# Network vectors on the common load queue, and a first result laid out by channel, sample and position

## The chip, the cores and the metric

The kernel runs on one core of one Trainium2 chip. The metric is the device time of one execution in microseconds (us), as a median of runs. The core has the engines PE (matrix products; PEld is its weight load), DVE, ACT and POOL (elementwise work), and SP, which here only issues transfers. ACT can issue transfers too. All transfers run on the same 16 DMA engines, and their queues are told apart in the profile as q1 (issued by SP), q10 (issued by ACT) and q8 (instructions).

## The reference

Two layers follow each other. Each normalizes its input over groups, makes a set of convolution weights of its own for every sample b and position l by a small network from z, applies them along l with three taps, and adds the input.

```python
S2, B, CI, CO, L, K, A, H = (32, 32, 64, 64, 256, 3, 16, 128)
h = jax.nn.relu(_ln(z @ W1 + b1, g1, be1))
w = (h @ W2 + b2).reshape(B, L, CI, CO, K)
hb = jax.nn.relu(_ln(z @ Wb1 + bb1, gb1, beb1))
bias = (hb @ Wb2 + bb2).transpose(0, 2, 1)
...
out = jnp.einsum('sbilk,bliok->sbol', x_uf, w)
out = out + bias[None]
...
x = x + _L0_conv_ref(_gn(x), ...)
x = x + _L1_conv_ref(_gn(x), ...)
```

`_gn` takes mean and variance over 32 groups of positions, across b and all channels. So layer 1 cannot normalize anything before all of layer 0's result is there. Everything is float32.

## The kernel before

**Tiling.** A unit u is one b of one layer: u = 0 to 31 is layer 0, u = 32 to 63 layer 1. A chunk v = 2u + h is half of a unit's output channels, so a layer has 64 chunks. In each chunk PE first makes the convolution weights (`make`, L390 and L391: the network's vectors `hT` of the unit against the table `w2`), DVE and ACT move them with their bias to `wall` (`take`, L401 and L416), and later PE multiplies them with the normalized input `xn` (`products`, L433). The products of a chunk stand on PE behind the first `make` of the following chunk. DVE adds the products to the residual (L442), in layer 0 it also takes statistics of the sum (L445), and the result is stored.

**What is loaded for each chunk, and in what order.** `after(v)` stands behind the products of chunk v. It issues on SP: the store of the chunk (layer 0: four transfers to `x1`, L367, in runs of 64 numbers, 256 B; layer 1: one to `out`, L372); the residual of chunk v + 2 (`load_residual`; layer 0: one transfer, L140; layer 1: four from `x1`, L143, in runs of 256 B); the next half of a unit's input, two channels by position parity in layer 0 (`load_pairs`, L128, runs of 8 KB) and twice 64 channels in layer 1 (L131, and L132 shifted by one position; runs of 1024 and 1020 B); and the bias of chunk v + 2 spread over samples (`load_bias`, L354, four transfers, runs of 8 KB). In between, POOL normalizes the half that was loaded before (L380, two instructions) and adds the bias to the residual of chunk v + 1 (L361). `load_pairs` waits for the first of these in layer 1, and `load_bias` for the last, since there is one buffer of each.

**`hT`.** The vectors of unit u + 1 are loaded by ACT (L116) at the head of chunk 2u, two buffers in turn. ACT executes in order, so the transfer is issued when ACT has done all `take` work of chunk 2u - 1.

**Completion counters.** Each transfer of SP and ACT signals one of eight semaphores, DMAHW0 to DMAHW7, which the scheduler deals out in turn over both queues. Before a transfer is issued, its engine waits until the transfer that had the same semaphore before (eight earlier in the scheduler's order) is complete.

## Time and profile before

| | us |
|---|---|
| median of 3 runs | 4618.15 (4603.26 to 4620.66) |
| profiled execution | 4594.6 |
| its span on the core | 4592.5 |
| first statistics and networks | to about 295 |
| first store of layer 0 (L367) | 328.20 |
| first store of layer 1 (L372) | 2400.46 |
| last two stores of layer 1, first of them | 4558.35 |

The span starts with the first instruction. A place in time is given in us from there. "Issue" as the cause of a wait means that the engine waited for nothing that the profile shows. PEclk is the share of the full clock that PE was granted. A chunk is told by the time from one chunk's first store to the next one's, since SP issues one group of stores a chunk.

### The profile page before, as it was taken

Reading aid. Unit: us, or ns where it says so; the run is one execution under the profiler, and the core shown is the slowest. Engines: PE = TensorE matmul, PEld = TensorE weight load, DVE = VectorE, ACT = ScalarE, POOL = GpSimd, SP = SyncE. Lnnn points to the kernel's source line nnn. Section 1 sums busy time; section 2 is a strip of 40 time slices with the busy share of each in tenths; the row PEclk is TensorE's granted clock in tenths of the full one; section 3 lists DMA queues with packets and bytes.
Section 4 is the critical chain, followed back from the end, with each engine's and each line's share of the span. In section 5 each row is a group of like instructions: output and inputs, shape, how many; then the busy total and the mean of one; then the engine's idle time right before and its main releaser. Section 6 shows DMA issues by size and latency. Waiting matters only on the chain.

```text
span 4592.5 us, 193878 instructions
## 1 busy us (share of the span) xinstructions
PE 4069.4 (89%) x90704; PEld 3883.6 (85%) x90704; DVE 2642.2 (58%) x3168; ACT 1291.2 (28%) x4264; POOL 2074.9 (45%) x618
## 2 busy tenths in 40 slices
PE   6889999999999999999969888888888888888888
PEld 3569999999999988899868888888888888888888
DVE  6876666666666666666645454545444554454455
ACT  3432232332322322223222222222222222222222
POOL 3465544455444554445344353353443533534532
PEclk9689999999999999999989999999999999999999
DMA  8874444445444454444567667576576675765764
GB/s 307 330 239 133 142 142 133 133 133 148 146 142 124 124 150 142 130 126 133 160 162 165 143 151 170 134 166 152 134 173 141 153 169 134 168 157 137 174 148 107
DMA packets 760621, 718.23 MB, mean 156 GB/s; under 512 B 567492, under 2 KB 715016, under 8 KB 716296
## 3 DMA queue, kind: packets, MB, share of 16 engines
q1 hardware_dynamic: 724488, 683.80, 56.5%
q10 hardware_dynamic: 35328, 22.03, 1.7%
q8 instruction: 709, 11.62, 1.1%
q14 instruction: 96, 0.79, 0.1%
HBM read 558.93 MB, written 146.80 MB: 154 GB/s over the span
## 4 chain that ended last, share of the span: by engine, by line
PE 82%; issue 9%; DVE 3%; DMA 3%; POOL 2%; ACT 1%; ACTq 0%; SPq 0%; POOLq 0%; DVEq 0%
PE pg L390 48%; PE pc L433 23%; PE pg L391 10%; DVE wall L401 2%; POOL sq L198 1%; DMA bd<-bs 1%; PE p L186 1%; DMA zt<-in_L_conv_z_dram 1%; DVE parts L445 1%; DVE room L442 1%; DMA room<-x 1%; PE p L226 0%; ACT ht L216 0%; ACT sq L190 0%; PE p L213 0%
## 5 line engine op out<-in xcount | busy, mean ns | idle before, releaser
L391 PE MATMUL pg<-hT,w2t 128*64 128x128 f32 x24576 | 2808.4, 278 | 60.7 <-issue 60.6
L390 PE MATMUL pg<-hT,w2t 128*64 128x128 f32 x24576 | 2808.6, 278 | 56.5 <-issue 48.2
L390 PEld LDWEIGHTS pg<-hT,w2t 128*64 128x64 f32 x24576 | 2758.8, 140 | 82.3 <-issue 61.9
L391 PEld LDWEIGHTS pg<-hT,w2t 128*64 128x64 f32 x24576 | 2759.2, 140 | 60.7 <-issue 60.7
L401 DVE TENSOR_TENSOR wall<-pg,b 128x1024 f32<-128x1024 f32 (+1 forms) x1536 | 1869.0, 1220 | 870.7 <-PE pg L391 866.8
L416 ACT ACTIVATE wall<-pg,b 64x128 f32<-64x128 f32 x4096 | 1176.7, 481 | 3090.3 <-DVE wall L401 2224.6
L380 POOL TENSOR_TENSOR xn<-room,gmean 128x2048 f32<-128x2048 f32 x128 | 606.6, 4739 | 2205.5 <-DMA room<-x 1104.4
L433 PE MATMUL pc<-wall,xn 128*32 128x128 f32 (+2 forms) x40960 | 1047.4, 261 | 313.3 <-issue 288.9
L433 PEld LDWEIGHTS pc<-wall,xn 128*32 128x32 f32 x40960 | 988.9, 114 | 379.1 <-issue 351.9
L442 DVE TENSOR_TENSOR room<-pc,room 128x512 f32<-128x512 f32 x512 | 354.1, 692 | 1002.4 <-PE pc L433 883.7
L380 POOL TENSOR_TENSOR xn<-xn,rstd 128x2048 f32<-128x2048 f32 x128 | 782.5, 6113 | 10.0
L361 POOL TENSOR_TENSOR room<-room,bt 128x2048 f32<-128x2048 f32 x128 | 593.4, 4636 | 82.3 <-DMA bt<-bd 72.3
L445 DVE BATCH_NORM_STATS2 parts<-room 128x6 f32<-128x256 f32 x512 | 192.9, 418 | 8.7
L198 POOL TENSOR_TENSOR sq<-sq 128x512 f32<-128x512 f32 (+2 forms) x192 | 103.6, 540 | 156.1 <-ACT sq L190 143.6
L186 PE MATMUL p<-wc,zt 17*128 17x256 f32 x256 | 99.8, 553 | 39.3 <-DMA zt<-in_L_conv_z_dram 39.3
L186 PEld LDWEIGHTS p<-wc,zt 17*128 17x128 f32 x256 | 67.5, 277 | 63.1 <-issue 39.7
L213 PEld LDWEIGHTS p<-ident,hs 128*128 128x128 f32 x256 | 50.2, 223 | 49.9 <-issue 49.9
L226 PE MATMUL p<-ht,Wb 128*64 128x512 f32 x64 | 56.7, 985 | 20.5 <-ACT ht L216 20.2
L213 PE MATMUL p<-ident,hs 128*128 128x128 f32 x256 | 62.7, 426 | 3.7 <-DVE hs L204 3.7
L287 DVE BATCH_NORM_STATS2 parts<-xn 128x6 f32<-128x256 f32 x192 | 64.0, 409 | 0.0
L287 DVE BATCH_NORM_STATS2 parts<-spare 128x6 f32<-128x256 f32 x160 | 53.5, 412 | 0.0
L287 DVE BATCH_NORM_STATS2 parts<-room 128x6 f32<-128x256 f32 x160 | 53.5, 412 | 0.0
(44 smaller groups left out, 231.4 us busy)
## 6 DMA issues: line engine op xcount, KB each, us to landing
bt<-bd SPq DMA_DIRECT2D x512, 256.0 KB, 8.9
room<-in_xp_dram SPq DMA_DIRECT2D x64, 1024.0 KB, 8.2
room<-in_xs_dram SPq DMA_DIRECT2D x64, 1024.0 KB, 6.4
x<-room SPq DMA_DIRECT2D x256, 256.0 KB, 4.2
room<-x SPq DMA_DIRECT2D x64, 1024.0 KB, 9.2
room<-x SPq DMA_DIRECT2D x256, 256.0 KB, 5.4
out_dram<-room SPq DMA_DIRECT2D x64, 1024.0 KB, 5.9
room<-x SPq DMA_DIRECT2D x64, 1020.0 KB, 12.9
```

The source lines that it names most:

```text
L186: nc.tensor.matmul(self.p1[:, k], self.zt[:, k * P : (k + 1) * P], self.t["wc"], start=True, stop=True)
L198: nc.gpsimd.tensor_tensor(to, self.sq[:, :, 0:w], self.sq[:, :, w : 2 * w], ALU.add)
L287: nc.vector.bn_stats(parts[:, g, u, h, :], xv[q % NX][:, j, :, g * E : (g + 1) * E])
L361: nc.gpsimd.tensor_tensor(y, y, bts.pop(v), ALU.add)
L380: nc.gpsimd.tensor_tensor(o, i, b, op)
L390: nc.tensor.matmul(pg[0:C, k, :], w[:, k0 * C : (k0 + 1) * C], h0, start=True, stop=True)
L391: nc.tensor.matmul(pg[C:P, k, :], w[:, k1 * C : (k1 + 1) * C], h1, start=True, stop=True)
L401: nc.vector.tensor_tensor(place(rows, a), pg[rows].rearrange("p o (t m) -> p t m o", t=NT), b2[n][rows, kind, None, None, o0 : o0 + OG].to ...
L416: nc.scalar.activation(place(rows, 0)[:, :, :, k], pg[rows, k].rearrange("p (t m) -> p t m", t=NT), AF.Identity, bias=b2[n][rows, kind, o0 ...
L433: nc.tensor.matmul(pc[t * S : (t + 1) * S, n0 - q * EB : n1 - q * EB, :], xn[:, u % 2, t * MT + p + 1, :], wall[:, t, a : a + (n1 - n0) * CH],
L442: nc.vector.tensor_tensor(part, pc.rearrange("p n o -> p o n"), part, ALU.add)
L445: nc.vector.bn_stats(parts[:, 2 * q + g, u, h, :], part[:, :, g * E : (g + 1) * E])
```

## The change

The `hT` transfer moves from ACT's queue to SP's, and from the head of chunk 2u (for unit u + 1) to `after(2u + 1)` (for unit u + 2), behind the residual loads and ahead of `load_pairs`. The first two units are loaded ahead of the loop. `x1` is laid out as channel, sample, position instead of sample, channel, position. Layer 1's `load_pairs` then reads 64 runs of 16 KB (the second transfer 4 B less, shifted by one number) instead of 1024 runs of about 1 KB. The last number of each sample's shifted row is then the next sample's first; it stands at an odd position, and `normalize` in layer 1 reads even ones only. The stores to `x1` and the residual loads keep their runs of 256 B, with 32 KB between consecutive channels and 1 KB between samples, where it was 1 KB and 64 KB.

```diff
-    x1 = [dram.tile([S, C, L], FP, name=f"x1_{b}") for b in range(B)]
+    x1 = [dram.tile([C, S, L], FP, name=f"x1_{b}") for b in range(B)]
...
     def load_hidden(u):
         h = hp.tile([P, 2, M], FP, tag="hT", name="hT")
-        nc.scalar.dma_start(out=h, in_=hd[u // 2][u % 2].rearrange("p (a m) -> p a m", a=2))
+        nc.sync.dma_start(out=h, in_=hd[u // 2][u % 2].rearrange("p (a m) -> p a m", a=2))
...
-            src = x1[u - B][k * SH : (k + 1) * SH].rearrange("s c l -> c s l")
+            src = x1[u - B][:, k * SH : (k + 1) * SH, :].rearrange("c s l -> c (s l)")
+            t = t.rearrange("p s l -> p (s l)")
             nc.sync.dma_start(out=t[0:C], in_=src)
-            nc.sync.dma_start(out=t[C:P, :, 0 : L - 1], in_=src[:, :, 1:L])
+            nc.sync.dma_start(out=t[C:P, 0 : SH * L - 1], in_=src[:, 1 : SH * L])
...
-                    in_=x1[u - B][:, h * CH : (h + 1) * CH, t * LT : (t + 1) * LT],
+                    in_=x1[u - B][h * CH : (h + 1) * CH, :, t * LT : (t + 1) * LT].rearrange("o s l -> s o l"),
...
-                        out=x1[u][:, h * CH : (h + 1) * CH, t * LT : (t + 1) * LT],
+                        out=x1[u][h * CH : (h + 1) * CH, :, t * LT : (t + 1) * LT].rearrange("o s l -> s o l"),
...
+            if h == 1 and u + 2 < U:
+                hs[u + 2] = load_hidden(u + 2)
             if v + 1 == NH * B:
...
-        hs[0] = load_hidden(0)
+        for u in range(2):
+            hs[u] = load_hidden(u)
...
-            if h == 0 and u + 1 < U:
-                hs[u + 1] = load_hidden(u + 1)
```

How this moves instructions. First SP in layer 0, before, from the input load of one chunk to the residual load of the next; behind each transfer stand the semaphores that it waits for.

```order
L128 DMA room<-in_xp_dram 128x2048 [waits DMAHW0_49,Pool_49]
L354 DMA bt<-bd_146 32x2048 [waits DMAHW2_49,DMAHW1_49,Pool_49]
L354 DMA bt<-bd_146 32x2048 [waits DMAHW3_49]
L354 DMA bt<-bd_146 32x2048 [waits DMAHW4_49]
L354 DMA bt<-bd_146 32x2048 [waits DMAHW5_49]
L367 DMA x_20_92<-room 32x32x64 [waits DMAHW6_49,DVE_49]
L367 DMA x_20_92<-room 32x32x64 [waits DMAHW7_49]
L367 DMA x_20_92<-room 32x32x64 [waits DMAHW0_49]
L367 DMA x_20_92<-room 32x32x64 [waits DMAHW1_49]
L140 DMA room<-in_xs_dram 128x2048 [waits DMAHW2_49]
```

The turn goes 0, 1, (2), 3, 4, 5, 6, 7, 0, 1, 2: the four bias loads have 1, 3, 4 and 5, and the 2 between them went to ACT's `hT`. So the residual load at the end, whose turn is 2 again, waits until that `hT` transfer is complete. On ACT, before, there are 64 pieces of `take` work (two chunks) between one `hT` and the next:

```order
L116 DMA hT<-hd_109 128x256
L416 ACTIVATE wall<-pg,b_0_184 64x4x32 x64
L116 DMA hT<-hd_109 128x256
L416 ACTIVATE wall<-pg,b_0_184 64x4x32 x64
L116 DMA hT<-hd_110 128x256
```

After the change ACT has none of these transfers in the loop, and on SP, in the same stretch of layer 0, from the residual load of one chunk to that of the next, it reads:

```order
L141 DMA room<-in_xs_dram 128x2048 [waits DMAHW6_49]
L116 DMA hT<-hd_114 128x256 [waits DMAHW7_49,PE_49]
L128 DMA room<-in_xp_dram 128x2048 [waits DMAHW0_49,Pool_49]
L355 DMA bt<-bd_146 32x2048 [waits DMAHW1_49,Pool_49]
L355 DMA bt<-bd_146 32x2048 [waits DMAHW2_49]
L355 DMA bt<-bd_146 32x2048 [waits DMAHW3_49]
L355 DMA bt<-bd_146 32x2048 [waits DMAHW4_49]
L368 DMA x_20_92<-room 32x32x64 [waits DMAHW5_49,DVE_49]
L368 DMA x_20_92<-room 32x32x64 [waits DMAHW6_49]
L368 DMA x_20_92<-room 32x32x64 [waits DMAHW7_49]
L368 DMA x_20_92<-room 32x32x64 [waits DMAHW0_49]
L141 DMA room<-in_xs_dram 128x2048 [waits DMAHW1_49]
```

The turn is whole on SP, and the residual load waits for the first bias load, eight transfers earlier on its own queue. `hT` itself waits for PE: its buffer was last read by the `make` of chunk 2u + 1. In layer 1, SP before, from one chunk's store to its input loads:

```order
L372 DMA out_dram<-room 128x2048 [waits DMAHW6_49,DVE_49]
L143 DMA room<-x_14_86 32x32x64 [waits DMAHW7_49]
L143 DMA room<-x_14_86 32x32x64 [waits DMAHW0_49]
L143 DMA room<-x_14_86 32x32x64 [waits DMAHW1_49]
L143 DMA room<-x_14_86 32x32x64 [waits DMAHW2_49]
L131 DMA room<-x_15_87 64x16x256 [waits DMAHW3_49,Pool_49]
L132 DMA room<-x_15_87 64x16x255 [waits DMAHW4_49]
```

And after the change, in a chunk that also loads `hT`:

```order
L373 DMA out_dram<-room 128x2048 [waits DMAHW2_49,DVE_49]
L144 DMA room<-x_12_84 32x32x64 [waits DMAHW3_49]
L144 DMA room<-x_12_84 32x32x64 [waits DMAHW4_49]
L144 DMA room<-x_12_84 32x32x64 [waits DMAHW5_49]
L144 DMA room<-x_12_84 32x32x64 [waits DMAHW6_49]
L116 DMA hT<-hd_126 128x256 [waits DMAHW7_49,PE_49]
L132 DMA room<-x_13_85 64x4096 [waits DMAHW0_49,Pool_49]
L133 DMA room<-x_13_85 64x4095 [waits DMAHW1_49]
```

`hT` stands ahead of the two input loads, and these have lost a dimension: 64 rows of 4096 and 4095 numbers.

## The prediction

> **What bounds the kernel now.** I read the page's busy time and chain first, then what PE waits for, stage by stage.

> ```profile
> PE 4069.4 (89%) x90704; PEld 3883.6 (85%) x90704; DVE 2642.2 (58%) x3168; ACT 1291.2 (28%) x4264; POOL 2074.9 (45%) x618
> PE 82%; issue 9%; DVE 3%; DMA 3%; POOL 2%; ACT 1%; ACTq 0%; SPq 0%; POOLq 0%; DVEq 0%
> PE   6889999999999999999969888888888888888888
> ...
> q8 instruction: 709, 11.62, 1.1%
> ```

> PE is the bound. Beside its own work the chain holds 9% "issue", in which PE waits for nothing that the profile shows. PE is less busy (8 instead of 9 tenths) in the second half, layer 1. The waits of PE, in two windows of 59 chunks of layer 0 and 58 of layer 1, first the windows' sums:

> ```profile
> 451.74:2330.92 1879.18, 1749.08 (x41526) 1711.33 (x41522) 1197.99 (x1422) 549.33 (x1894) 868.50 (x171) 0.97 0.47 137
> 2462.01:4500.89 2038.88, 1770.52 (x40842) 1725.65 (x40840) 1005.62 (x929) 526.98 (x1856) 884.62 (x175) 0.95 0.67 154
> ```
> ```profile
> PE pc L433 <- issue: 119.4, 50, 6.3
> ...
> PE pc L433 <- issue: 159.9, 96, 6.1
> PE pg L391 <- issue: 60.6, 24, 4.5
> PE pg L390 <- issue: 47.6, 17, 4.6
> ```

> Columns of the windows: length, busy time (and count) of PE, PEld, DVE, ACT, POOL, then the granted clock, the DMA share and GB/s. A chunk has 704 matmuls, so 41526 and 40842 are 59 and 58 chunks: **31.85 us a chunk in layer 0, 35.15 in layer 1**. The first wait row is layer 0's, the other three are layer 1's: 119 and 268 us. The DMA engines are busy 0.47 of the time in layer 0 and 0.67 in layer 1.

> What is "issue"? In layer 1's products:

> ```profile
> 3147.03 1.74 PE L433 MATMUL pc<-wall,xn 128*32 128x32 f32 x63
> 3150.14 2.86 PE L433 MATMUL pc<-wall,xn 128*32 128x128 f32 x128 [1.38 <-issue]
> 3159.10 5.06 PE L433 MATMUL pc<-wall,xn 128*32 128x128 f32 x129 [6.09 <-issue]
> ```

> PE stops every 128 matmuls. PE has 2 x 90704 records and q8 moved 11.62 MB, so about 64 B an instruction; 128 matmuls with their 128 weight loads are 16.4 KB, which is also q8's mean packet (11.62 MB / 709). So I read these stops as PE waiting for its next packet of instructions, late because the 16 DMA engines are full of the kernel's own transfers. Products use up a packet in 2.9 us, `make` in about 6 (60 matmuls in 3 us, in the last row of the rates below), so a burst of transfers hurts most when it meets products.

> When do the bursts come? SP's waits (first row layer 0's window, second layer 1's), then SP's queue over two chunks of layer 1, and ACT's `hT`:

> ```profile
> SPq L140 <- DMA hT<-hd: 481.7, 28, 18.0
> ...
> SPq L143 <- DMA hT<-hd: 595.0, 29, 22.4
> ```
> ```profile
> 3093.29 0.36 SPq L372 DMA_DIRECT2D out_dram<-room  x1
> 3093.70 23.09 SPq L143 DMA_DIRECT2D room<-x  x4
> 3116.89 2.17 SPq L131 DMA_DIRECT2D room<-x  x1
> ...
> 3120.31 2.90 SPq L354 DMA_DIRECT2D bt<-bd  x4
> 3123.31 0.37 SPq L372 DMA_DIRECT2D out_dram<-room  x1
> 3123.72 15.95 SPq L143 DMA_DIRECT2D room<-x  x4
> ```
> ```profile
> 3111.91 0.33 ACTq L116 DMA_DIRECT2D hT<-hd  x1
> ```

> Once a unit, the residual loads wait 17 to 21 us on average for an `hT` that ACT issues only behind two chunks of its own work (3111.91). The semaphores dealt out in turn over both queues make this wait, no data does. In these 20 us the DMA engines lie idle beside `make`; then everything is issued at once (3116.9 to 3123.7) into the products and on top of the next chunk's load. What that costs is seen by single chunks:

> ```profile
> 362.28:392.22 29.94, 28.92 (x708) 27.99 (x706) 20.16 (x24) 9.59 (x32) 29.78 (x6) 1.00 0.49 143
> ...
> 422.04:451.74 29.70, 28.98 (x710) 28.08 (x706) 20.16 (x24) 9.61 (x32) 29.54 (x6) 1.00 0.49 144
> 1206.64:1238.56 31.92, 28.85 (x706) 28.13 (x702) 20.15 (x24) 9.04 (x32) 1.10 (x2) 0.99 0.47 136
> 1238.56:1268.52 29.96, 29.96 (x712) 29.75 (x712) 20.34 (x24) 9.41 (x32) 29.80 (x6) 0.95 0.50 146
> 2432.20:2462.01 29.81, 28.91 (x705) 28.06 (x701) 17.34 (x17) 9.09 (x32) 23.03 (x5) 1.00 0.80 179
> 3093.29:3123.31 30.02, 29.48 (x726) 29.06 (x722) 18.28 (x17) 9.06 (x32) 5.21 (x2) 1.00 0.41 104
> 3123.31:3164.92 41.61, 30.22 (x692) 29.11 (x690) 16.40 (x17) 9.05 (x32) 26.01 (x6) 0.92 0.84 185
> 4500.89:4529.36 28.47, 28.47 (x710) 28.22 (x708) 17.33 (x17) 9.06 (x32) 11.20 (x3) 1.00 0.48 113
> ```

> The first two rows are the first and last of three chunks of layer 0 before a residual load first waits for an `hT`: 29.82 us on average. From then on they alternate, in the middle of the layer 31.92 and 29.96. Chunk 2432.20 is the key: layer 1, **all 5 MB of its transfers, none held back, 29.81 us**. With the same transfers piled up, the pair at 3093.29 takes 30.02 + 41.61. The last row, with no input load (POOL and DMA nearly idle later on), is layer 1's floor: 28.47.

> SP's queue in the key chunk:

> ```profile
> 2432.20 0.36 SPq L372 DMA_DIRECT2D out_dram<-room  x1
> 2432.60 6.84 SPq L143 DMA_DIRECT2D room<-x  x4
> 2439.55 1.03 SPq L131 DMA_DIRECT2D room<-x  x1
> ...
> 2446.95 1.92 SPq L354 DMA_DIRECT2D bt<-bd  x4
> ```

> **The change part by part.**

> *`hT` on SP.* The wait of the residual loads goes, in all chunks after the first few. I take the observed chunks for what is left: layer 0 59 x (31.85 - 29.82) = **120 us**, layer 1 58 x (35.15 - 29.81) = **310 us**. A check from the other side: at the three early chunks' PE busy time of 28.9 the layer-0 window would have 59 x 28.9 = 1705 instead of 1749 (44 less, the time at a reduced clock), and 79 or so of 119 us of issue go (at 0.7 a chunk left): 123. What is late next: in layer 0 DVE (20.16 busy of 29.8), since 29.82 holds it already; in layer 1 products meet the tail of the bias load, which 29.81 holds too. What it adds: 64 issues on SP of 0.33 us behind the residual loads, covered as long as SP has gaps (5 us ahead of the bias loads in the key chunk). `hT` now waits for PE at chunk 2u + 1's `make`; that stands ahead of the products whose result the store ahead of it on SP already waited for, so it adds nothing for the input and bias loads behind it. It is there over a unit ahead of its use. If that cover were gone, PE would stop for a landing of about 2 us.

> *16 KB runs.* Rates, by windows with one kind of transfer each: 8 KB runs into 128 partitions, 8 KB runs into 32 (the bias), 256 B stores, and the 1 KB loads into 64 partitions:

> ```profile
> 1230.00:1234.00 4.00, 3.80 (x169) 3.53 (x160) 3.38 (x9) 0.00 (x0) 0.00 (x0) 1.00 1.01 424
> 1255.00:1258.00 3.00, 3.00 (x60) 3.00 (x58) 2.13 (x2) 1.35 (x6) 2.92 (x2) 1.00 1.07 232
> 1209.00:1212.00 3.00, 2.80 (x52) 2.56 (x50) 2.06 (x3) 1.89 (x8) 0.00 (x0) 1.00 0.89 219
> 2443.00:2446.00 3.00, 3.00 (x60) 3.00 (x56) 1.95 (x3) 2.27 (x8) 3.00 (x1) 1.00 1.07 206
> ```

> The 2.1 MB of a chunk's input take 10.2 us at 206 GB/s. The new shape is in no row. It is between 232 (long runs, few partitions: 9.0 us) and 424 (long runs, all partitions: 4.9 us). I take the nearer, 232, since 256 B, 1 KB and 8 KB runs all give 206 to 232 where a transfer covers a part of the partitions: 1.2 us fewer of DMA in a chunk, of which I count **0**, because they fall beside `make`. At 424 the transfers would end ahead of the products, and a chunk would come near the floor.

> [...]

> *The pitch of the 256 B runs.* Same bytes and runs at other addresses; the trace has no such row. The nearest slow one also writes 256 B runs, in the first stage (the second row; the first is the store to `x1`; size and median us to landing):

> ```profile
> x<-room SPq DMA_DIRECT2D x256, 256.0 KB, 4.2
> ...
> bd<-bs ACTq DMA_DIRECT2D x32, 128.0 KB, 9.2
> ```

> It lands 5 us later, at half the size; at that price layer 1's bias, behind these loads, would end 5 us later and reach into the products, which is rival 2's time. The other end is 424 GB/s, rival 1's. I take 219 and 0 us, since three very different patterns share 206 to 232 and the slow row is from another stage. SP's issue of the input loads has 64 rows instead of 1024 (1.03 us before, 0.36 for a store of 128 rows): about 1 us of SP, hidden.

> **Sum.** 120 + 310 + 2 (the first chunk of layer 1) = 432 us. The profiled execution took 4594.6 (span 4592.5), so 4162.6. It is 0.5% below the median of the runs, 4618.15; scaled by that ratio: **4184 us**.

> **Rivals.**
> 1. *The input arrives at the full rate* (424 GB/s). For: run length grows 16-fold. Against: 8 KB runs at 232. Layer 1 at its floor, 28.47: 58 x 6.68 = 387, with 122 from the rest 509; 4594.6 - 509 = 4086, scaled 4107.
> 2. *Only half of layer 1's piling goes*, because input and bias are still issued together and reach into the products (5 MB need 23 of 30 us). For: DMA share 0.80 in the key chunk. Against: that chunk itself. At 32 us a chunk: 183 + 122; 4290, scaled 4312.
> 3. *Long runs hold instruction packets up.* If a DMA engine finishes a long run before it turns to q8, PE stops in `make` too. The input lasts 9 us, 1.5 packets of `make`, so two stops a chunk; layer 1's longest stop in `make` is 4.6. At that price 29.8 + 9.2 = 39.0: layer 1 loses 223, layer 0 gains 120, 4698, scaled **4722, slower**. It decides from 35.15 + 120/58 = 37.2 us a chunk, 3.7 us a stop. For: nothing here ran 16 KB runs beside `make`. Against: 8 KB runs beside it cost nothing (chunk 422.04, 1.00 clock). At half the price: 34.4, about 4450.
> 4. *It isn't when, it is how much*: PE's stops depend on the bytes, which don't change, and the time stays at 4618. For: layer 1 has more bytes and more stops. Against: key chunk. [...]

> **How the numbers follow.** Chances: forecast 0.52, rival 1 0.20, rival 2 0.12, rival 3 0.05 at full and 0.04 at half price, rival 4 0.07. The forecast's own spread is 4154 to 4230 (29.3 to 30.6 us a chunk in layer 1). The range reaches from below rival 1 to rival 2, **4095 to 4315**, and leaves out 16% and tails. Faster by over 0.5% (23 us, about what a measurement here can tell): 0.52 + 0.20 + 0.12 + 0.04 = 0.88; slower 0.05; the same 0.07.

> **What would show it.** Right: no wait of residual loads for `hT` in SP's waits; chunks evenly 29.5 to 30 us in both layers; issue waits of PE under 50 us in each window; clock 0.99 or more. 16 KB step: the windows with input loads alone say 232 or 424. Rival 3 would show as issue waits at L390 and L391 while the input is loaded; rival 2 as waits at L433 beside a late bias load. I am wrong if even chunks still have stops.

## The result, and the profile after

| | before | after |
|---|---|---|
| median, us | 4617.26 (4603.26 to 4620.66, 4 runs) | 4304.34 (4300.02 to 4309.94, 4 runs) |
| ratio, 95% interval | | 0.9328 [0.9306, 0.9351] |
| span of the profiled execution, us | 4592.5 | 4303.7 |

The kernel is 6.7% faster. The spans differ by 288.8 us. By the first stores of chunks, as before, they come from these stretches:

| stretch | before, us | after, us | difference |
|---|---|---|---|
| to the first store of layer 0 | 328.20 | 325.39 | -2.8 |
| next four chunks | 123.54 | 120.87 | -2.7 |
| 59 chunks of layer 0 | 1879.18 | 1765.19 | -114.0 |
| to the third store of layer 1 | 131.09 | 139.59 | +8.5 |
| 58 chunks of layer 1 | 2038.88 | 1861.82 | -177.1 |
| rest | 91.6 | 90.8 | -0.8 |

A chunk of layer 0 now takes 1765.19 / 59 = **29.92 us**, a chunk of layer 1 1861.82 / 58 = **32.10 us**. First the page of the changed kernel, busy time and chain:

```profile
PE 3955.2 (92%) x90704; PEld 3758.3 (87%) x90704; DVE 2637.9 (61%) x3168; ACT 1294.4 (30%) x4264; POOL 2083.3 (48%) x618
PE 82%; issue 6%; DVE 6%; DMA 2%; POOL 2%; ACT 1%; SPq 0%; ACTq 0%; POOLq 0%; DVEq 0%
```

"Issue" fell from 9% to 6% of the chain, and PE is 114 us less busy at the same number of matmuls, while the granted clock in the two windows rose from 0.97 and 0.95 to 1.00. The two windows of the changed kernel (length, busy time and count of PE, PEld, DVE, ACT, POOL, granted clock, DMA share, GB/s):

```profile
446.26:2211.45 1765.19, 1713.94 (x41526) 1666.57 (x41522) 1190.31 (x1416) 550.62 (x1888) 871.50 (x171) 1.00 0.52 148
2351.04:4212.86 1861.82, 1696.69 (x40838) 1648.63 (x40835) 1005.65 (x929) 527.51 (x1856) 889.10 (x175) 1.00 0.73 168
```

PE's waits in them (total us, times, longest), the first row layer 0's, the others layer 1's:

```profile
PE pc L434 <- issue: 37.9, 74, 2.6
...
PE pc L434 <- issue: 143.8, 138, 2.5
PE pg L392 <- issue: 11.3, 14, 1.3
PE pg L391 <- issue: 9.9, 12, 1.8
```

Layer 0's issue went from 119 to 38 us. Layer 1's went from 268 to 165; the waits in `make` fell to a fifth (108 to 21), those in the products are more in number and shorter (96 of 1.7 us on average before, 138 of 1.0 us now). SP's waits in layer 1:

```profile
SPq L373 <- DVE room L443: 1081.6, 59, 22.0
SPq L355 <- POOL room L362: 148.2, 29, 5.4
SPq L116 <- PE pg L392: 23.6, 28, 1.1
```

No residual load waits for `hT` any more. SP waits where it has nothing to do yet (the store, for its data), and `hT` waits for PE 0.8 us a time. So the wait that the change was to remove is gone in every unit, and yet layer 1 keeps over half of its issue. One chunk shows how, first SP's queue, then every microsecond from the end of `make`:

```profile
3089.85 0.36 SPq L373 DMA_DIRECT2D out_dram<-room  x1
3090.25 6.78 SPq L144 DMA_DIRECT2D room<-x  x4
3097.13 0.99 SPq L116 DMA_DIRECT2D hT<-hd  x1
3098.22 0.45 SPq L132 DMA_DIRECT2D room<-x  x1
3098.72 0.59 SPq L133 DMA_DIRECT2D room<-x  x1
3104.57 1.71 SPq L355 DMA_DIRECT2D bt<-bd  x4
```
```profile
3102.00:3103.00 1.00, 1.00 (x22) 1.00 (x20) 0.72 (x1) 1.00 (x6) 1.00 (x1) 1.00 1.05 213
3103.00:3104.00 1.00, 1.00 (x22) 1.00 (x20) 0.76 (x1) 0.33 (x2) 1.00 (x1) 1.00 1.03 213
...
3111.00:3112.00 1.00, 0.85 (x30) 0.58 (x22) 0.00 (x0) 0.00 (x0) 0.03 (x1) 1.00 0.99 213
3112.00:3113.00 1.00, 0.00 (x0) 0.00 (x0) 0.00 (x0) 0.00 (x0) 1.00 (x1) 1.00 1.02 229
3113.00:3114.00 1.00, 0.19 (x8) 0.19 (x12) 0.00 (x0) 0.00 (x0) 1.00 (x1) 1.00 0.76 156
3114.00:3115.00 1.00, 1.00 (x41) 1.00 (x37) 0.32 (x1) 0.00 (x0) 1.00 (x1) 0.57 0.22 57
3115.00:3116.00 1.00, 1.00 (x28) 0.92 (x20) 0.37 (x1) 0.00 (x0) 1.00 (x1) 0.50 0.02 8
```

The transfers begin at once and in good order, and the 16 DMA engines are full for 23 us, to 3114 (a share of 0.90 to 1.11 in the windows from 3090 to 3113). `make` ends near 3110. The products run into the tail of the bias load, PE stops for 2 us (3111.9 to 3113.8), and then works some 3 us at a clock of 0.57 to 0.50. The first two rows, between the landing of the residual and the issue of the bias, show the input load in its 16 KB runs: 213 GB/s.

### The profile page after: what moved, and what is told of

The parts are those of the page before. It is cut to its first block, busy times and chain, and to the rows that moved or that the text cites. A ratio compares the mean times of both kernels' runs of the same rounds, so it can differ in the third digit from the quotient of the medians.

```text
span 4303.7 us, 193876 instructions
## 1 busy us (share of the span) xinstructions
PE 3955.2 (92%) x90704; PEld 3758.3 (87%) x90704; DVE 2637.9 (61%) x3168; ACT 1294.4 (30%) x4264; POOL 2083.3 (48%) x618
## 3 DMA queue, kind: packets, MB, share of 16 engines
q8 instruction: 709, 11.62, 1.2%
## 4 chain that ended last, share of the span: by engine, by line
PE 82%; issue 6%; DVE 6%; DMA 2%; POOL 2%; ACT 1%; SPq 0%; ACTq 0%; POOLq 0%; DVEq 0%
PE pg L391 52%; PE pc L434 23%; PE pg L392 6%; DVE wall L402 3%; POOL sq L199 1%; DMA zt<-in_L_conv_z_dram 1%; DVE parts L446 1%; DVE room L443 1%; PE p L187 1%; POOL xn L381 1%; DMA room<-x 1%; ACT ht L217 0%; ACT sq L191 0%; DMA hd<-ht 0%; DMA xn<-in_xs_dram 0%
## 5 line engine op out<-in xcount | busy, mean ns | idle before, releaser
L391 PE MATMUL pg<-hT,w2t 128*64 128x128 f32 x24576 | 2729.0, 273 | 22.1 <-issue 11.1
L392 PE MATMUL pg<-hT,w2t 128*64 128x128 f32 x24576 | 2729.3, 273 | 11.9 <-issue 11.7
L391 PEld LDWEIGHTS pg<-hT,w2t 128*64 128x64 f32 x24576 | 2677.4, 137 | 45.4 <-DVE wall L402 24.8
L392 PEld LDWEIGHTS pg<-hT,w2t 128*64 128x64 f32 x24576 | 2677.4, 137 | 16.8 <-issue 16.7
L434 PE MATMUL pc<-wall,xn 128*32 128x128 f32 (+2 forms) x40960 | 1017.5, 255 | 218.0 <-issue 191.0
L434 PEld LDWEIGHTS pc<-wall,xn 128*32 128x32 f32 x40960 | 949.0, 111 | 294.3 <-issue 266.3
## 6 DMA issues: line engine op xcount, KB each, us to landing
bt<-bd SPq DMA_DIRECT2D x512, 256.0 KB, 10.2
x<-room SPq DMA_DIRECT2D x256, 256.0 KB, 4.3
room<-x SPq DMA_DIRECT2D x256, 256.0 KB, 6.1
```

The source lines that it names most:

```text
L391: nc.tensor.matmul(pg[0:C, k, :], w[:, k0 * C : (k0 + 1) * C], h0, start=True, stop=True)
L392: nc.tensor.matmul(pg[C:P, k, :], w[:, k1 * C : (k1 + 1) * C], h1, start=True, stop=True)
L434: nc.tensor.matmul(pc[t * S : (t + 1) * S, n0 - q * EB : n1 - q * EB, :], xn[:, u % 2, t * MT + p + 1, :], wall[:, t, a : a + (n1 - n0) * CH],
```

## The experiments

Layer 0 and layer 1 below are the mean times of a chunk in the profiled execution, by first stores, where 31.85 and 35.15 stand for before and 29.92 and 32.10 for the change. All ratios are to the kernel before, run on the same chip.

| | median, us | ratio, 95% interval | layer 0, us | layer 1, us |
|---|---|---|---|---|
| e1 `hT` alone | 4301.69 | 0.9317 [0.9299, 0.9335] | 29.96 | 31.90 |
| e2 layout alone | 4622.23 | 1.002 [1.0001, 1.0039] | 31.87 | 35.35 |
| e3 two ahead, ACT's queue | 4463.77 | 0.9667 [0.9648, 0.9685] | 30.21 | 34.55 |
| e4 1020 B runs | 4318.69 | 0.935 [0.9332, 0.9369] | 30.02 | 32.18 |
| e5 no bias loads in layer 1 | 4225.01 | 0.9166 [0.9134, 0.9199] | 29.90 | 30.72 |
| e6 1 MB more a chunk | 4354.90 | 0.9454 [0.9427, 0.9481] | 30.77 | 32.0 |
| e7 2 MB more a chunk | 4536.45 | 0.9849 [0.9814, 0.9884] | 33.59 | 31.94 |
| e8 second copy, shifted | 4598.80 | 0.9984 [0.9966, 1.0003] | 37.33 | 29.03 |
| e9 two equal copies | 4248.79 | 0.92 [0.9176, 0.9223] | 30.43 | 30.51 |
| e10 the change again | 4312.06 | 0.9329 [0.9305, 0.9354] | 30.04 | 32.12 |
| e11 e9, bias first | 4177.14 | 0.9053 [0.9034, 0.9071] | 30.37 | 29.29 |
| e12 the change, bias first | 4339.85 | 0.9398 [0.938, 0.9416] | 29.97 | 32.63 |

### Which part of the change does it: e1, e2, e3, e4

e1 is the kernel before with `hT` as in the change:

```diff
-        nc.scalar.dma_start(out=h, in_=hd[u // 2][u % 2].rearrange("p (a m) -> p a m", a=2))
+        nc.sync.dma_start(out=h, in_=hd[u // 2][u % 2].rearrange("p (a m) -> p a m", a=2))
...
+            if h == 1 and u + 2 < U:
+                hs[u + 2] = load_hidden(u + 2)
...
-        hs[0] = load_hidden(0)
+        for u in range(2):
+            hs[u] = load_hidden(u)
...
-            if h == 0 and u + 1 < U:
-                hs[u + 1] = load_hidden(u + 1)
```

> The kernel before with hT alone moved to SP, two units ahead; x1 keeps its layout and the input loads their 1 KB runs. Theory A (the run length is worth nothing, since 64-partition loads stay at 206 to 232 GB/s, and layer 1's 32.1 us a chunk come from the bias load's tail meeting the products): within 0.5% of the full change, 4290 to 4325 us, layer 1 at 32 us a chunk. Theory B (the 16 KB runs hold PE's instruction packets up and give part of the gain back): 29.8 us a chunk in layer 1 as in the one unhindered chunk of before, so some 130 us less than the full change, 4150 to 4200 us. Theory C (the long runs do help): slower than the full change, above 4330 us.

e2 is the change with those same lines put back to what they were, so that only the layout and the runs differ.

> The full change with hT left where it was (ACT, one unit ahead). Theory A: the residual loads keep their wait of about 20 us for hT and the piled transfers their stops: within 0.5% of before, 4595 to 4640 us. Theory B: slower than before by up to 2.3 us a chunk of layer 1, 4640 to 4750 us. Theory C: faster than before, under 4590 us.

Measured: e1 0.9317, the change 0.9328, and their intervals overlap; e2 1.002. **All of the gain is `hT`'s, none of it the layout's.** e2 alternates in layer 1 between 29.80 and 40.9 us, and SP waits there as before, now at L144:

```profile
SPq L144 <- DMA hT<-hd: 582.9, 29, 22.0
```

e3 keeps `hT` two chunks ahead, but issues it on ACT's queue:

```diff
-        nc.sync.dma_start(out=h, in_=hd[u // 2][u % 2].rearrange("p (a m) -> p a m", a=2))
+        nc.scalar.dma_start(out=h, in_=hd[u // 2][u % 2].rearrange("p (a m) -> p a m", a=2))
```

> The full change, but hT stays on ACT's queue, issued at the new place (two units ahead, behind the first piece of take work). Tells the place from the queue. If the late issue behind two chunks of ACT's work was what held SP, the early place alone mends it: 4290 to 4325 us, no SP wait for hT above 2 us. If semaphores shared by two queues hold SP whatever the place, a wait for hT stays in SP's list and the time lies between the two kernels, 4400 to 4600 us.

Measured: 4463.77, half of the gain. SP's waits in layer 0 and in layer 1 (one window each), and one chunk's bias loads on SP's queue:

```profile
SPq L368 <- DMA hT<-hd: 742.6, 28, 27.2
...
SPq L355 <- DMA hT<-hd: 666.5, 26, 27.1
```
```profile
3201.42 27.41 SPq L355 DMA_DIRECT2D bt<-bd  x4
```

Nobody needs this `hT` soon, and SP still waits 27 us for it, because a transfer of SP's has its semaphore next in turn. With the transfer's new place in the program the turn falls on the store (layer 0) and the bias load (layer 1) instead of the residual load. In layer 0, where it is the store that waits, this costs little (30.21 us a chunk); the loss is layer 1's (34.55). So the harm lies in one turn over two queues of which one lags, not in how early the data are wanted.

e4 is the change with layer 1's input read in 1020 B runs from the new layout:

```diff
-            src = x1[u - B][:, k * SH : (k + 1) * SH, :].rearrange("c s l -> c (s l)")
-            t = t.rearrange("p s l -> p (s l)")
-            nc.sync.dma_start(out=t[0:C], in_=src)
-            nc.sync.dma_start(out=t[C:P, 0 : SH * L - 1], in_=src[:, 1 : SH * L])
+            src = x1[u - B][:, k * SH : (k + 1) * SH, :]
+            nc.sync.dma_start(out=t[0:C, :, 0 : L - 1], in_=src[:, :, 0 : L - 1])
+            nc.sync.dma_start(out=t[C:P, :, 0 : L - 1], in_=src[:, :, 1:L])
```

> The full change with layer 1's input loaded from the new layout in runs of 1020 B again (16 a row; the first transfer leaves out each sample's last, unread number too). Theory A: as the full change, 4290 to 4325 us. Theory B: 4150 to 4200 us. With e1 it also tells the layout's pitch: if e1 and this one differ by over 0.5%, the stores and residual loads at the new pitch do.

Measured: 0.935, against 0.9328 and, in a second measurement, 0.9329 for the change. With 16 times as many runs the layer-1 chunk takes 32.18 instead of 32.10 us. The two intervals overlap. Run length makes no difference here that these runs can tell, in either direction.

### What is left in layer 1: e5, e6, e7

The forecast had 29.81 us for a layer-1 chunk. Two theories for the 32.10: only the part of a chunk's transfers that runs on after `make` costs, or every microsecond of DMA time does. e5 takes 1 MB away; its layer 1 loads no bias and uses the last one of layer 0, so that its output differs:

```diff
+            if u >= B:
+                bts[v] = kept[0]
+                return
-            bts[v] = bp.tile([P, CH, LT], FP, tag="bt", name="bt")
+            bts[v] = kept[0] = bp.tile([P, CH, LT], FP, tag="bt", name="bt")
```

> The full change with layer 1's bias loads left out (the last bias of layer 0 is added again and again), 1 MB and some 4.5 us of DMA fewer a chunk of layer 1. Theory A (layer 1's 32.1 us a chunk come from 23 us of transfers that begin with make and end in the products): the transfers then end beside make, a chunk of layer 1 falls to 28.5 to 29.3 us, the whole to 4304 - 58 x 3 = 4100 to 4150 us. Theory D (the stops grow with the bytes, wherever they fall): 1 of 5 MB fewer takes a fifth of the 3.4 us above the floor, 31.4 us a chunk, 4250 to 4275 us.

Measured: 30.72 us a chunk, between the two. PE's waits in its layer 1, two-microsecond windows of one chunk whose transfers began at 3086, PE's row after the stop, and the packets of the queues from 3099 to 3104 and (last row) from 3104 to 3105:

```profile
PE pc L438 <- issue: 74.6, 123, 1.5
```
```profile
3100.00:3102.00 2.00, 2.00 (x42) 2.00 (x40) 1.48 (x2) 0.00 (x0) 0.00 (x0) 1.00 1.15 238
3102.00:3104.00 2.00, 2.00 (x42) 2.00 (x40) 1.47 (x2) 1.58 (x7) 0.00 (x0) 1.00 0.75 152
3104.00:3106.00 2.00, 2.00 (x40) 2.00 (x36) 1.30 (x2) 0.69 (x3) 0.00 (x0) 1.00 0.07 16
3106.00:3108.00 2.00, 1.32 (x42) 1.01 (x43) 0.00 (x0) 0.00 (x0) 0.00 (x0) 1.00 0.00 0
```
```profile
3106.87 0.27 PE L395 MATMUL pg<-hT,w2t 128*64 128x128 f32 x1 [0.68 <-issue]
```
```profile
q1 hardware_dynamic: 78, 1.00, 95.2%
q14 instruction: 1, 0.01, 0.8%
...
q8 instruction: 1, 0.02, 8.7%
```

The DMA engines are nearly idle from 3104 on, while `make` still runs, and PE nevertheless loses 0.7 us at 3106, in the last matmuls of `make`. So a tail in the products isn't needed for a stop. The rows of the queues show why: while the engines were full no instruction packet came through on q8 in these 5 us, and the first one went as soon as they were free. PE's row follows 2.6 us behind it. The packets are followed one by one below.

e6 and e7 add DMA time to layer 0, one or two stores of 1 MB a chunk to a place that nobody reads (here e7's):

```diff
+    extra = [dram.tile([C, SH * L], FP, name=f"extra_{i}") for i in range(8)]
...
+            if 0 <= v and u < B - 1:
+                for i in range(2):
+                    nc.sync.dma_start(out=extra[(2 * v + i) % 8], in_=w2[0:C, 0:22, :].rearrange("p o k -> p (o k)")[:, 0 : SH * L])
```

> The full change with one more store of 1 MB a chunk of layer 0 (from 64 partitions, 16 KB runs, right behind the residual load, to a scratch area in DRAM). Layer 0 then moves 5 MB a chunk as layer 1 does, but begins and ends it beside make (15.5 + 5 of about 20 us). Theory A: next to nothing, up to 0.5 us a chunk, 4304 to 4335 us. Theory D: layer 0 gets layer 1's 2.2 us of extra stops a chunk, 4420 to 4450 us.

> As the run with 1 MB more, with two such stores a chunk of layer 0 (25 us of transfers against 20 us of make). Theory A: the tail now meets the products, 2 to 3 us a chunk more than the full change, 4420 to 4480 us. Theory D: twice the 1 MB run's loss.

Measured: layer 0 takes 0.85 us a chunk longer with 1 MB and 3.67 us with 2 MB. Both theories missed: A had up to 0.5 us for the first and 2 to 3 for the second, D had 2.2 us for the first and twice its loss for the second. The cost is not proportional: the second megabyte costs 2.8 us, over three times the first. That speaks against a fixed price per byte. PE's waits between 460 and 2200 us (some 57 chunks of e6, 52 of e7), e6 and then e7:

```profile
PE pc L436 <- issue: 71.9, 123, 2.1
```
```profile
PE pc L436 <- issue: 157.9, 101, 4.1
```

### A faster load: e8, e9, e10

Both keep two copies of the first result in DRAM, so that layer 1 reads its input in one load over 128 partitions instead of two over 64. In e8 the second copy is stored shifted by one number:

```diff
+        o = shift * (C * ROW - 1) + h * CH * ROW + t * LT
...
-            nc.sync.dma_start(out=t[0:C], in_=src)
-            nc.sync.dma_start(out=t[C:P, 0 : SH * L - 1], in_=src[:, 1 : SH * L])
+            nc.sync.dma_start(out=t[:, 0 : SH * L - 1], in_=x1[u - B][:, k * SH * L : (k + 1) * SH * L - 1])
...
+                for shift in range(2):
+                    for t in range(NT):
+                        nc.sync.dma_start(
+                            out=x1_at(u, shift, h, t),
+                            in_=residual(v)[t * S : (t + 1) * S],
+                        )
```

> The full change with x1 kept twice in DRAM, the second copy shifted by one number, so that layer 1 loads a half unit with one transfer over all 128 partitions. Layer 0 stores 1 MB more a chunk (256 B runs, about 4.7 us of DMA), layer 1's input should take 4.9 instead of 9.8 us at 424 GB/s. Theory A: layer 1 falls to 28.5 to 29.5 us a chunk, layer 0 stays within 0.6 us, in all 4110 to 4190 us. If the rate is set by something other than the partitions covered, the input stays at 10 us and the time at 4304 or above.

Measured: layer 1 falls to 29.03 us as theory A had it, layer 0 rises to 37.33, where it had at most 0.6 us more, and the whole stays at 0.9984. PE's waits between 2800 and 4400 us, and three windows: the input load alone, the stores of the aligned copy, and those of the shifted one:

```profile
PE pc L439 <- issue: 17.7, 39, 1.0
```
```profile
3313.00:3317.00 4.00, 4.00 (x78) 4.00 (x76) 2.95 (x3) 2.27 (x8) 4.00 (x2) 1.00 0.95 390
1304.00:1308.00 4.00, 4.00 (x78) 4.00 (x76) 2.53 (x3) 1.87 (x8) 0.00 (x0) 1.00 0.97 231
1309.00:1315.00 6.00, 6.00 (x116) 6.00 (x112) 4.14 (x4) 2.63 (x10) 0.00 (x0) 1.00 1.42 77
```

The same bytes arrive at 390 GB/s instead of 213 when the load covers all 128 partitions. The stores shifted by 4 B run at 77 GB/s, a third of the 231 of the aligned copy, whose rows e8 pads in the same way. They cost layer 0 59 x 7.41 = 437 us against the change, over twice the 58 x 3.07 = 178 that layer 1 gains.

e9 stores the second copy at the same alignment and lets `normalize` take the even numbers of one and the odd numbers of the other, with one more instruction on POOL:

```diff
+                for a in range(2):
+                    rows = slice(a * C, (a + 1) * C)
+                    i = pairs(u, k)[rows, :, a::2].rearrange("p s (g e) -> p s g e", g=G)
+                    nc.gpsimd.tensor_tensor(o[rows], i, spread(gmean, rows), ALU.subtract)
...
-                for t in range(NT):
+                for a in range(2):
+                    for t in range(NT):
```

> The full change with x1 kept in two equal, aligned copies, so that layer 1 loads a half unit with one transfer over 128 partitions; normalize then takes the even positions from the first 64 partitions and the odd ones from the others (one more POOL instruction of about 4.7 us a chunk of layer 1). Theory A: layer 1 as in the run with the shifted second copy, 29.0 us a chunk (58 x 3.1 = 178 us fewer than the full change), layer 0 as in the run with 1 MB more of stores, 0.85 us a chunk more (50 us): 4160 to 4200 us, faster than both kernels. If the second copy's stores are as slow aligned as they were shifted, layer 0 stays at 37 us a chunk and the time near 4600.

> The full change again, on the same chip as the run with two aligned copies, for a direct comparison: 4290 to 4320 us.

Measured: 4248.79, 1.5% under the change itself, which ran beside it (e10, 4312.06), but above the 4160 to 4200 of theory A: layer 1 took 30.51 us and not 29.0. The aligned second copy costs layer 0 some 0.4 us a chunk (30.43 against e10's 30.04), where the shifted one cost 7.3. Layer 1 takes 28.92 us in one kind of chunk and 32.1 in the other. SP's queue in the slow kind, and POOL's work beside it:

```profile
3031.60 0.36 SPq L372 DMA_DIRECT2D out_dram<-room  x1
3040.49 0.34 SPq L131 DMA_DIRECT2D room<-x  x1
3051.13 1.72 SPq L353 DMA_DIRECT2D bt<-bd  x4
```
```profile
3030.89 9.58 POOL L389 TENSOR_TENSOR xn<-room,gmean 64x2048 f32<-64x2048 f32 x2 [21.06 <-PE pc L442]
3040.54 6.04 POOL L390 TENSOR_TENSOR xn<-xn,rstd 128x2048 f32<-128x2048 f32 x1
3046.53 4.58 POOL L360 TENSOR_TENSOR room<-room,bt 128x2048 f32<-128x2048 f32 x1
```

The two subtracts of 64 partitions take as long each as one of 128 (4.7 us in either kernel), the bias is added behind them, and the load of the next bias, which waits for that, is issued 19.5 us into the chunk: into the products.

### The order of the bias: e11, e12

In layer 1 the bias is added and loaded ahead of the normalizing of the next pairs, in e11 with e9's copies, in e12 with the change's layout:

```diff
-            if w != B:
+            if u < B and w != B:
                 next_pairs(w, k)
             if v + 1 < NH * U:
                 add_bias(v + 1)
             if v + 2 < NH * U:
                 load_bias(v + 2)
+            if u >= B:
+                next_pairs(w, k)
```

> As e9 (the input in two equal copies, read in one load of 128 partitions), and in layer 1 the sum of the bias and the bias load stand ahead of the normalizing of the next pairs on POOL, so that the bias load no longer follows POOL's two slower subtracts of every second chunk. Theory 1 (a chunk is late by the DMA time that still runs when its products begin): the bias load ends some 4 to 7 us sooner in every chunk, both kinds of chunk take about 29 us in layer 1 (e9: 28.92 and 32.1), layer 0 stays at 30.4, and the time is 4150 to 4190 us. Rival (only the amount of DMA time counts, not its place in the chunk): the amount is that of e9, the mean stays at 30.5 us a chunk and the time at 4249 within 15. Rival 2 (the normalizing, now later on POOL, holds the products): PE shows waits for POOL, and the time is above 4249.

> The changed kernel with the same reordering of layer 1 alone: the sum of the bias and the bias load ahead of the normalizing of the next pairs on POOL; the layout and the loads are those of the change. Here the input loads, the state loads and the bias load together fill about 23 us of a chunk of 32. If only the amount of DMA time counts, the bias load comes sooner and the input load behind it ends as late as before: 32.1 us a chunk, 4304 within 15. If the place of the bias load behind POOL is what makes it late, the chunk loses 1 to 2 us of its 32.1, and the time is 4200 to 4270 us.

Measured, e11: **4177.14 us, 0.9053 [0.9034, 0.9071]**, the fastest of all, with 29.10 and 29.48 us in the two kinds of chunk, as theory 1 had it. e11's layer 1, PE's waits and the last microseconds of a chunk's transfers, which began at 3111.4:

```profile
PE pc L442 <- issue: 27.9, 53, 1.0
```
```profile
3130.00:3131.00 1.00, 1.00 (x24) 1.00 (x22) 1.00 (x1) 0.07 (x1) 1.00 (x1) 1.00 0.98 410
3131.00:3132.00 1.00, 1.00 (x37) 0.83 (x37) 0.21 (x1) 0.00 (x0) 1.00 (x1) 1.00 0.19 66
```

They end at 3131.2, as the products begin. The same DMA work as in e9 costs 58 x (30.51 - 29.29) = 71 us less when it ends there; the medians differ by 72 (the two ran on different chips; by their ratios it is 68). It is the place that counts, then, and not the bytes alone.

e12 came out where neither expectation had it: 4339.85, and 0.9398 [0.938, 0.9416] is slower than the change's [0.9306, 0.9351]. Its layer-1 window, and one chunk whose transfers began at 3102.5:

```profile
2353.64:4246.82 1893.18, 1717.11 (x40852) 1674.61 (x40850) 1005.99 (x929) 526.02 (x1856) 893.56 (x175) 0.98 0.72 166
...
3124.00:3125.00 1.00, 0.12 (x5) 0.00 (x0) 0.00 (x0) 0.00 (x0) 0.00 (x0) 1.00 0.97 197
3125.00:3126.00 1.00, 0.00 (x0) 0.00 (x0) 0.00 (x0) 0.00 (x0) 0.00 (x0) 1.00 0.55 115
3126.00:3127.00 1.00, 0.00 (x0) 0.00 (x0) 0.00 (x0) 0.00 (x0) 0.00 (x0) 1.00 0.06 16
3127.00:3128.00 1.00, 0.81 (x41) 0.81 (x45) 0.07 (x1) 0.00 (x0) 0.00 (x0) 1.00 0.00 0
3128.00:3129.00 1.00, 1.00 (x33) 1.00 (x29) 0.62 (x1) 0.00 (x0) 0.97 (x1) 0.65 0.05 16
3129.00:3130.00 1.00, 1.00 (x27) 1.00 (x21) 0.00 (x0) 0.00 (x0) 1.00 (x1) 0.50 0.00 0
```

Whatever stands first, the transfers of this layout end some 23 us into the chunk, as in the change. Here PE stops for 3.1 us in one piece, and then the clock is down. Of the 31.4 us that the window is longer than the change's, 20.4 are PE busy time (1717.11 against 1696.69) at the same number of matmuls. So reordering helps only where the transfers then end in time.

The number of q8's packets in the first 20 us of a chunk, roughly the length of `make`, over 50 chunks of layer 1 of each kernel (a chunk needs 5.5 in all):

| | q8 packets in the first 20 us | us a chunk |
|---|---|---|
| e12 | 2.44 | 32.63 |
| the change | 2.58 | 32.10 |
| e5 | 2.82 | 30.72 |
| e9 | 2.98 | 30.51 |
| e11 | 3.18 | 29.29 |

Among these five, the fewer packets come in during `make`, the longer the chunk. The count alone is no rule, though: layer 1 of the kernel before has 3.1 at 35.15 us, layer 0 of the change 2.6 at 29.92.

The traces tell more when each packet is set against the instructions that it brings. q8's 709 packets of 16,384 B are 11.62 MB, and PE has 181,408 matmuls and weight loads: 64 B an instruction, 256 to a packet (709 x 256 = 181,504). In all fourteen profiled runs every "issue" wait of PE, 3309 of them, falls at the same place in a group of 256 instructions, and PE goes on in the median 1.4 us after the packet for the next group has landed. **So these waits are waits for instruction packets.** Where PE has caught up with its packets and the DMA engines are free, a packet's transfer starts some 1.1 us after PE has begun the packet before it and takes 1 us, and the first instruction follows 1.2 to 1.6 us later: about 3.5 us from packet to packet (in the change PE begins one at 3049.78, the next is on its way from 3050.89 to 3052.06, and PE begins it at 3053.25). That is enough in `make`, where a packet lasts 7.0 us (the prediction had about 6), and too long in the products, where one lasts 2.9. (Where PE still has instructions in hand the transfer starts sooner, and no stop follows: in the floor chunk of before, 4500.89, the last two started 0.25 us before and 0.5 us after PE had begun the packet ahead of them.) With the engines full the start came up to 6.5 us after PE had begun the packet before (the change). In e5 the packet of the stop at 3106 started at 3104.27, 5.3 us after PE had begun the one before.

This divides the 165 us of stops in layer 1 of the change: 132 us (110 stops) had a packet that started over 1.4 us after its predecessor's first instruction, the other 33 us (54 stops) one that started in time. In e11 the late packets make 6 us (9 stops), the others 25 (51). So e11 has removed nearly all that the transfers cost in stops, and what it keeps is the way of the packets themselves. No run shows a large reserve that a quiet stretch fills up for later: by this count, in the chunks of no run had more than 503 instructions, two packets, landed ahead of PE.

## Why the prediction held, and where it didn't

**Direction, and the wait that goes: right.** The time, 4304, lies in the range, near its upper end, 120 us above the forecast of 4184. It is inside only because the range was drawn out to rival 2, which had a chance of 0.12; the forecast's own spread, 4154 to 4230, missed. SP's wait for `hT` is gone, e1 puts the whole gain on that, and e3 shows that it is the shared turn of the semaphores that made it: with the transfer wanted two chunks later but still on ACT's queue, SP waits as long as ever (742.6 and 666.5 us in the two layers' windows, against 481.7 and 595.0 before). One sign that the prediction named against itself came true, "even chunks still have stops": the chunks of layer 1 are even now, and 164 stops stay. It had also asked for under 50 us of issue in each window; layer 0 has 38, layer 1 has 165. Its reading of "issue" as a wait for instruction packets holds for every such wait.

**Layer 0, 59 x (31.85 - 29.82) = 120 us: right.** Measured 114; the chunk takes 29.92.

**Layer 1, 58 x (35.15 - 29.81) = 310 us: the step that failed.** It measured 58 x (35.15 - 32.10) = 177, and these 133 us are nearly all of the 143 by which the sum, 432, missed the 289 of the spans (the rest: 6 in layer 0, and 10.5 in the transition between the layers, which got 8.5 slower where the sum had 2 us of gain, against some 6 won at the edges; 3.1 of the 8.5 are in the first two chunks of layer 1, 5.4 ahead of them, and their cause stays open). The mechanism was right and the size was taken wrongly: the step made one chunk, 2432.20, stand for a layer. None of the 58 chunks of the change is as short; they take 30.6 to 33.3 us. That chunk's transfers filled the DMA engines for 23 us as well, to 2455. But the instruction packet that met their tail started 2.6 us after PE had begun the one before, and PE didn't stop for it; in the change's chunk at 3089 it was 4.7 us, and PE stopped for 2. Why the packet came through sooner there stays open. A mean of the short chunks of before would not have helped either: e2 still shows 29.80 in every second chunk, but those, like the first chunk of the pair that the prediction quotes, have their input held back behind the `hT` wait until `make` is over. The sum of a steady chunk was at hand in rival 2 and was set aside for that chunk: 5 MB fill the DMA engines for about 23 us, and `make` lasts 20.

**Rival 2, "only half of layer 1's piling goes", at 32 us a chunk and 4312 us:** this is what happened, by size and mostly by its mechanism, input and bias together reaching into the products. The forecast argued against it from the same single chunk. e11 confirms it from the other side: with the transfers ending as the products begin, 29.29. e5 shows that it isn't all: 91 us of stops stay, and about half of them (43 us) had a packet that started in time.

**16 KB runs at 0, and the new pitch at 0: right.** 213 GB/s, below the 232 that was taken; e2 and e4 give no difference beyond 0.3%. Rival 1 (the input at the full rate) didn't come about through the change, but its price was sound: with the load over 128 partitions, 390 GB/s, layer 1 comes to 29.03 (e8), where the rival had 28.47.

**Rival 3 (long runs hold packets up): refuted.** e1 with 1 KB runs and the change with 16 KB runs have the same time, and the waits in `make` fell to 21 us instead of rising.

**Rival 4 ("not when, but how much"): refuted as a whole,** since e1 moves the same bytes as before and is 6.8% faster. What is true in it shows in e6 and e7: bytes count once they fill the stretch (0.85 us a chunk for the first megabyte, 2.8 for the second). The traces show no store of instructions that would cover a chunk: a chunk has about 1408, at most 503 lay ahead of PE in the chunks of any run, and layer 1 of the change still waits 165 us for packets.

## What to carry to other kernels

Where completion semaphores are dealt in turn over several queues, look for a transfer on a lagging engine's queue: here it held up SP's by up to 27.2 us at a time even when it was issued two chunks ahead (e3), and not at all from SP's own queue (e1, the change). Put it on the queue whose order it must keep. Don't take one good chunk for the steady state: add up the time for which the transfers fill the DMA engines, and compare it with the stretch in which PE uses its instruction packets slowly, here `make` with 7.0 us a packet. What shortens the transfers (all 128 partitions in one load) paid in full only together with an order that lets them end in time: a layer-1 chunk takes 32.10 us in the change, 30.51 with the shorter load (e9), 32.63 with the order alone (e12), 29.29 with both (e11).
